# A conv-attention layer and a mixture-of-experts layer in one kernel: branch to the end, one pool for both layers, norm factors by way of DRAM

## The chip, the cores and the metric

The kernel runs on one core of a Trainium2 chip. The metric is device microseconds of one execution. Of the engines, TensorE (PE) does the matrix products and transposes, VectorE (DVE) and ScalarE (ACT) the elementwise work, GpSimd (POOL) a little of it, and SyncE (SP) issues all DMAs from one queue, in program order.

## The reference

Eight images `x` of 256 channels by 32 x 32 pixels (1024 tokens) pass two layers, all in float32.

```python
# layer 0 (norm1, norm2: RMS over the channels, per pixel)
q, k, v = bn(conv1x1(rms(x), qkv_w))                  # 4 heads, q and k of 32, v of 64
a = softmax(q.T @ k * 32**-0.5)                       # per head, over 1024 keys
x = x + gamma1 * bn(conv1x1(v @ a.T + bn(dwconv3(v)), proj_w))
h = dwconv3(conv1x1(rms(x), pi_w))                    # 1024 channels
f = conv1x1(gelu(h[:512]) * h[512:], po_w)
x = x + gamma2 * irfft2(rfft2(f by 8x8 patches) * fft_p)
# layer 1, on tokens t = x transposed
z = layer_norm(t)
t = t + causal_softmax(z WQ^T (z WK^T)^T / 16) @ (z WV^T)
z = layer_norm(t)
w = softmax(mean_over_images(z) @ Wr + br)            # 8 experts, one weight per token
t = t + sum_e w_e * (relu(bn(relu(bn(z W1_e)) W2_e)) Wo_e)
```

## The kernel before

**Layer 0.** An image is a block of 128 partitions x 2 channel groups x 1024 tokens, called `t`. The parts of an image are generators that issue a few instructions at each step: `attend` (scores, exponentials, products), `project`, `norm2`, `hidden` (the first conv of the FFN and its depthwise taps), `mix` (the second conv), `spectrum` (the patch transforms, by products with fixed matrices, and the addition to `t`). While image b is in its attention, image b-1 is in its FFN. The order in which the steps of the generators alternate is written out by hand in four strings, one letter per step: `FIRST` for stage 0, `ORDER` for stages 1 to 6, `LAST` for stage 7, `TAIL` for the FFN of the last image. All instructions of PE, ACT, DVE and POOL pass through `InOrder` (so nearly all carry line 88) and keep the program's order; no scheduler moves them. A letter's place thus sets where an instruction stands in its engine's queue. In the strings `h` is a step of `hidden`, `a` of `attend`, `d` and `q` of the next image's norm and keys, `s` of `spectrum`, `n` of `norm2`. `ON_PE` names the channel groups of `hidden` whose taps run as diagonal products on PE and not on DVE.

**The norm's factors.** `rms_norm` (L565) works on halves of 512 tokens. The sum of squares becomes one factor per token, a column per 128 tokens; `factors` (L592) takes the root and splits the factor `a` into a rounded part and a rest, `turned` (L612) transposes both to rows `rT`, and `apply` (L618) spreads them over 128 partitions by four products with the selector `pick_n` into PSUM, tile `rbn`, and multiplies: `xn<-t,vec,rbn` on DVE.

**The softmax divisor.** `attend` (L761) goes by blocks c of 256 queries. `close` (L788) takes the sums `sm` over the keys into `ss`, `invert` the reciprocal `r`, tile `sr`; `split` (L801) makes `rh` and the rest `rl`, and `spread` (L805) brings them to the channels of each head by four products with `pick_r` into tile `rb`, with which `pu` is multiplied. The softmax does not subtract a maximum. For that reason sums and reciprocals are gathered in `accs`.

**The seam.** After the last image's `spectrum`, L1233 to L1239 test `accs` and leave the integer `bad`. Each engine loads it and branches: if it is set, `layer0_shifted` (L182) computes layer 0 again, with the maximum subtracted. Layer 1's pools are opened behind the branch.

**Layer 1.** `scores_matrix` (in `TAIL`) has folded WQ and WK to one matrix, stored to `at_d`. Behind the branch `load_t` reads the image back from `t_d`, `load_experts` (L1348) issues 24 weight loads, and `first_norm(0)`, `keys(0)` and `values(0)` run by themselves: sixteen transposes into `tpt` and eight `bn_stats`, the root on POOL, scaling, transposing back to `z`, then products `pk` and `pv`. From then on images overlap: `statistics` of the next image, whose factors `rmT` are stored to `rm_d` and read back over all partitions as `rb`, lie beside the causal scores `s<-kk,z` of the current one. The expert FFN follows, in halves of 512 tokens, PE with hardly a pause; of its eight experts the odd ones replace products of 2 x 2 blocks by seven.

Of the kernel before, what the change touches and what calls it, by code (L numbers as in the profile page):

```python
# [18 lines left out]
P = 128  # L19
# [32 lines left out]
for _name, _w in _VEC:  # L52
# [7 lines left out]
    "aahhahdhhahqahahqahdhqhhhahaqahhqaaqadqaaqaaaaqaqaqaqaaqaaahqkvrgvvrgvvgpvrvvggppppp"  # L60
)
ORDER = (
    "nhsnhhsndhhhnhssnhshahnhahhsnshshhshhssdhshhhhhhaadshhhqahhahqhhhdhhhhqhhhhhdqdhhhhqdhhh"
    "qhdhhhhqhhdhhhqhhhahhhqhdhdhhhhqhdhhhdhhqkhavhhrgvgrvgvgpvrpvvppgppv"
)
LAST = (
    "nhshnhhahsnhsanhhshshnanhahnshshhshahshsshahhahhssahahhhdhhdhhhahhhahhhhhhaahaahhhhahhha"
    "ahhaahhhhdahhhhhhhaahhhhahhahhhahahhhhhhphprgrhghrgppppg"
)
TAIL = (  # L70
    "nnsnssnsnsnsnhhshhhhshshxhhsshhhhshhxhhmhhhhhshhhxhhhhhhmhhmhhhhhhhhhhhhhhhhhhhhhhhhhxhh"
    "hh"
)

ON_PE = ((), (), (2,))
# [18 lines left out]
def conv_attn_hybrid_kernel(  # L94
# [352 lines left out]
    t = [None] * B  # L447
    with ExitStack() as l0:
# [7 lines left out]
        def load_x(b):  # L456
            t[b] = two.tile([P, KC, N], F32, tag="t", name="t", bufs=3)
            nc.sync.dma_start(t[b], xv[b])


        t[0] = two.tile([P, KC, N], F32, tag="t", name="t", bufs=3)
# [3 lines left out]
        qkvw = wpool.tile([P, KC, 2 * C], F32, name="qkvw")  # L465
# [46 lines left out]
        pick_n = wpool.tile([2 * nq, nq, P], F32R, name="pick_n")  # L512
# [13 lines left out]
        mhalf = const.tile([P, nq], F32, name="mhalf")  # L526
# [38 lines left out]
        def rms_norm(b, wname, xn, first=False):  # L565
# [26 lines left out]
            def factors(h):  # L592
# [11 lines left out]
                pool.tensor_tensor(a, y, mhalf, ALU.pow)  # L604
# [3 lines left out]
                pool.tensor_mul(a, a, y)  # L608
                pool.tensor_copy(r[:, 0, :].bitcast(F32R), a)
                pool.tensor_sub(r[:, 1, :].bitcast(F32R), a, r[:, 0, :])  # L610

            def turned(h):  # L612
                tr = ps_m.tile([2 * nq, P], F32, tag="mm", name="tr")
                pe.transpose(tr, r_of.pop(h).rearrange("p a b -> p (a b)"), ident)
                rT_of[h] = small.tile([2 * nq, P], F32R, tag="rT", name="rT", bufs=2)
                act.copy(rT_of[h], tr)

            def apply(h):  # L618
                rT = rT_of.pop(h)
                rb = ps_m.tile([P, HALF], F32, tag="mm", name="rbn")  # L620
                for i in range(nq):
                    pe.matmul(rb[:, i * P : (i + 1) * P], pick_n[:, i, :], rT, start=True, stop=True)
                hs = slice(h * HALF, (h + 1) * HALF)
                for k in range(KC):
                    dve.scalar_tensor_tensor(xn[:, k, hs], t[b][:, k, hs], col(wname, k), rb, ALU.mult, ALU.mult)
# [31 lines left out]
        def queries_keys(b):  # L657
# [8 lines left out]
            for g, h in ((0, 0), (1, 0), (1, 1), (0, 1)) if b == 0 else ((0, 0), (0, 1), (1, 0), (1, 1)):  # L666
                if g not in att[b]:
                    hi = one.tile([P, N], F32R, tag=f"hi{g}", name="hi")
                    lo = one.tile([P, N], F32, tag=f"lo{g}", name="lo")
                    att[b][g] = (hi, lo)  # L670
# [7 lines left out]
                if b == 0 and (g, h) == (1, 0):  # L678
                    st = att[b]["kst"] = one.tile([P, NH, N], F32R, tag="kst", name="kst")
                    for r in range(4):  # L680
                        eng, src = ((dve, hi.bitcast(F32)), (pool, lo))[r // 2]
                        for hd in range(NH):
                            eng.tensor_copy(
                                st[r * KD : (r + 1) * KD, hd, hs], src[hd * KD : (hd + 1) * KD, hs]
                            )
                elif b == 0:
                    stack(b, ((g, hs),))
                yield 1.7

        def stack(b, parts=((0, slice(0, N)), (1, slice(0, N)))):  # L690
            for g, part in parts:
                hi, lo = att[b][g]
                name = ("qst", "kst")[g]
                if name not in att[b]:
                    att[b][name] = one.tile([P, NH, N], F32R, tag=name, name=name)
                st = att[b][name]
                for r in range(4):
                    src = (hi, lo, hi, lo)[r] if g == 0 else (hi, hi, lo, lo)[r]
                    for hd in range(NH):
                        nc.sync.dma_start(  # L700
                            st[r * KD : (r + 1) * KD, hd, part].bitcast(F32),
# [3 lines left out]
        def values(b):  # L705


            vT = att[b]["vT"] = one.tile([P, NT, C], F32, tag="vT", name="vT")
# [40 lines left out]
        def v_conv(b):  # L749
            o = att[b]["o"] = one.tile([P, KC, N], F32, tag="o", name="o")  # L750
# [10 lines left out]
        def attend(b, at_once):  # L761
# [26 lines left out]
            def close(c, po, sm):  # L788
# [5 lines left out]
                rh = two.tile([P, QC], F32R, tag="rh", name="rh", bufs=1)  # L794
                rl = two.tile([P, QC], F32R, tag="rl", name="rl", bufs=1)
# [5 lines left out]
                def split():  # L801
                    act.activation(rh, r, AF.Copy, accum_out=accs[:, 1, b, c : c + 1])
                    pool.tensor_sub(rl, r, rh.bitcast(F32))

                def spread():  # L805
                    rb = ps_m.tile([P, NH // 2, QC], F32, tag="mm", name="rb")
                    for pair in range(NH // 2):
                        pe.matmul(rb[:, pair, :], pick_r[:, pair, :], rh, start=True, stop=False)
                        pe.matmul(rb[:, pair, :], pick_r[:, pair, :], rl, start=False, stop=True)
# [23 lines left out]
            while units:  # L833
# [3 lines left out]
                for c, j in now:  # L837
                    s = ps_s.tile([P, NH, QC], F32, tag="s", name="s")
                    for hd in range(NH):
                        pe.matmul(  # L840
                            s[:, hd, :], kst[:, hd, j * P : (j + 1) * P], qst[:, hd, c * QC : (c + 1) * QC], start=True, stop=True
# [191 lines left out]
        def spectrum(b):  # L1033
# [50 lines left out]
            if b + 3 < B:  # L1084
                load_x(b + 3)

# [109 lines left out]
        lin = one.tile([P, 4, KC, C], F32, tag="qst", name="lin")  # L1196
        for i, src in enumerate((wqT, wkT)):
            nc.sync.dma_start(lin[:, i], src.rearrange("(k p) o -> p k o", p=P))

        def scores_matrix():  # L1200
# [8 lines left out]
            for g in range(KC):  # L1209
# [4 lines left out]
            act.activation(lin[:, 0], pa, AF.Copy, scale=1.0 / math.sqrt(C))  # L1214
            nc.sync.dma_start(at_d, lin[:, 0])
            yield 1.7

# [7 lines left out]
                "x": groups_on_pe(B - 1, ON_PE[2]).__next__,  # L1225
            },
            TAIL,
        )
        for _ in spectrum(B - 1):
            pass  # L1230
# [10 lines left out]

    with tc.If(nc.values_load(bad[0:1, 0:1]) > 0):
        layer0_shifted()
# [7 lines left out]
    z_d = [dram.tile([P, KC, N], F32, tag=f"zd{b}", name=f"zd{b}") for b in range(B)]  # L1251
    u_d = [dram.tile([P, KC, N], F32, tag=f"ud{b}", name=f"ud{b}") for b in range(B)]
    wm = ctx.enter_context(tc.tile_pool(name="wm", bufs=1))
    wrs = wm.tile([P, KC, NE], F32, name="wrs")
    nc.sync.dma_start(wrs, wr.rearrange("(k p) e -> p k e", p=P))
    brs = wm.tile([1, NE], F32, name="brs")
    nc.sync.dma_start(brs, br)

    wT = wm.tile([4 * NE, N], F32R, name="wT")

    w_of = []
    for e in range(NE):
        w_of.append([])
        for name in ("w1", "w2", "wo"):
            w_ = wm.tile([P, KC, C], F32, tag=f"{name}_{e}", name=f"{name}_{e}")
            w_of[e].append(w_)

    nc.vector.tensor_scalar_mul(wrs, wrs, 1.0 / B)

    sel_ = wm.tile([4 * NE, NE, P], F32, tag="tz0", name="sel_")  # L1270
    nc.gpsimd.memset(sel_, 0.0)
    for half in range(2):
        nc.gpsimd.affine_select(
            out=sel_, in_=sel_, compare_op=ALU.not_equal, fill=1.0, base=-NE * half,
            pattern=[[-1, NE], [0, P]], channel_multiplier=1,
        )
    sel8 = wm.tile([4 * NE, NE, P], F32R, name="sel8")
    nc.gpsimd.tensor_copy(sel8, sel_)
    sums_of = [[None] * 3 for _ in range(NE)]

    def seven(e):

        return e % 2 == 1

    sums_d = dram.tile([NE, 3, P, 3, P], F32, name="sums_d")

    def weight_sums(space):


        for e in range(NE):  # L1290
            for l in (0, 1, 2) if seven(e) else (0, 2):
                w_ = w_of[e][l]
                if e == 0:
                    s_ = sums_of[e][l] = wm.tile([P, 3, P], F32, tag=f"ws{e}_{l}", name=f"ws{e}_{l}")
                else:
                    s_ = space.tile([P, 3, P], F32, tag="ws", name="ws", bufs=2)
                a11, a21, a12, a22 = (w_[:, k, g * P : (g + 1) * P] for k in range(KC) for g in range(KC))
                dve.tensor_add(s_[:, 0, :], a21, a22)
                yield
                dve.tensor_sub(s_[:, 1, :], s_[:, 0, :], a11)  # L1300
                yield
                dve.tensor_sub(a21, a11, a21)
                yield
                dve.tensor_sub(s_[:, 2, :], a12, s_[:, 1, :])
                if e:
                    nc.sync.dma_start(sums_d[e, l], s_)
                yield

    def column_sums(src, T):

        B4 = src.rearrange("p k (c n) -> p (k c) n", n=QC)
        dve.tensor_sub(T[:, 0:2, :], B4[:, 1::2, :], B4[:, 0:2, :])
        dve.tensor_add(T[:, 2, :], T[:, 1, :], B4[:, 0, :])
        dve.tensor_sub(T[:, 3, :], B4[:, 2, :], T[:, 2, :])
        return T

    feat_d = dram.tile([P, KC, HALF], F32, name="feat_d")

    def gate(h, sums, lg, rows_of):


        nt = NT // 2
# [775 lines left out]
```

## Time and profile before

| | us |
|---|---|
| median of 3 runs | 3111.69 (3111.09 to 3112.32) |
| profiled execution, whole time | 3112.39 |
| its span in the trace | 3110.4 |
| stage 0 of layer 0 (attention of image 0) | 48.36 to 149.40 |
| stage 1 | 149.40 to 289.92 |
| stages 2 to 6 | 146.55 each, 289.92 to 1022.70 |
| stage 7 | 1022.70 to 1169.00 |
| FFN of the last image | 1169.00 to 1286.00 |
| seam to layer 1's first scores | 1286.00 to 1326.30 |
| layer 1's attention | 1326.30 to 1877 |
| expert FFN and end | 1877 to 3110 |

A row of the stretches of time gives the window, its length, then the busy time and number of instructions of PE, PEld (the load of PE's stationary operand, beside the products), DVE, ACT and POOL, PE's granted clock as a share of full speed, the share of the DMA engines and their GB/s. A row of the timeline gives start, duration, engine, line and operation, with the tiles as out<-in, and in square brackets how long the engine stood idle and for what. Rows of the DMA issues give the queue, the number of issues, the size of one and the time from issue to landing. The busy shares of the whole span (PE 95%, DVE 79%) are means over stages with different limits, so stages have to be read one by one.

### The profile page before, as it was taken

Reading aid. Unit: us, or ns where it says so; the run is one execution under the profiler, and the core shown is the slowest. Engines: PE = TensorE matmul, PEld = TensorE weight load, DVE = VectorE, ACT = ScalarE, POOL = GpSimd, SP = SyncE. Lnnn points to the kernel's source line nnn. Section 1 sums busy time; section 2 is a strip of 40 time slices with the busy share of each in tenths; the row PEclk is TensorE's granted clock in tenths of the full one; section 3 lists DMA queues with packets and bytes.
Section 4 is the critical chain, followed back from the end, with each engine's and each line's share of the span. In section 5 each row is a group of like instructions: output and inputs, shape, how many; then the busy total and the mean of one; then the engine's idle time right before and its main releaser. Section 6 shows DMA issues by size and latency. Waiting matters only on the chain. (4 is left out here: it accounts for less than half of the span.)

```text
span 3110.4 us, 42740 instructions
## 1 busy us (share of the span) xinstructions
PE 2968.0 (95%) x17008; PEld 2023.4 (65%) x17008; DVE 2444.3 (79%) x3796; ACT 1411.8 (45%) x2187; POOL 333.0 (11%) x486
## 2 busy tenths in 40 slices
PE   7989999999999989599999988999999999999998
PEld 4555555656565645356656656778887777788877
DVE  4398989898989897556676655888888878888887
ACT  4556556565656553132223323444444444444443
POOL 2131111111111100012222320000000000000000
PEclk9999999999999999799999998999999999999999
DMA  3202020203021100402222213000000000000000
GB/s 117 55 1 55 28 55 28 57 27 82 7 77 30 40 8 17 138 34 96 81 80 93 84 55 106 21 21 21 21 28 21 21 21 21 21 21 21 21 8 14
DMA packets 52293, 136.22 MB, mean 44 GB/s; under 512 B 7750, under 2 KB 20726, under 8 KB 46454
## 3 DMA queue, kind: packets, MB, share of 16 engines
q1 hardware_dynamic: 52086, 133.41, 13.6%
q8 instruction: 136, 2.23, 0.3%
q14 instruction: 71, 0.58, 0.1%
HBM read 62.88 MB, written 37.99 MB: 32 GB/s over the span
## 5 line engine op out<-in xcount | busy, mean ns | idle before, releaser
L88 ACT ACTIVATE h<-h,bn_o,bn_s 128x512 f32<-128x512 f32 x384 | 308.6, 813 | 627.8 <-DVE h L88 627.7
L88 ACT ACTIVATE pT<-s 128x1024 f32<-128x1024 f32 x256 | 260.7, 1024 | 193.4 <-PE sums L88 133.7
L88 DVE SCALAR_TENSOR_TENSOR conv<-hpad,vec,conv 128x1024 f32<-128x1024 f32 x256 | 333.0, 1306 | 6.1
L88 DVE SCALAR_TENSOR_TENSOR x<-hpad,vec,x 128x1024 f32<-128x1024 f32 x248 | 317.6, 1286 | 16.3 <-ACT x L88 9.9
L88 PE MATMUL pm<-h,w 128*128 128x512 f32 (+1 forms) x768 | 321.6, 528 | 0.0
L88 PE MATMUL po<-pT,vT 128*32 128x256 f32 x4096 | 274.8, 386 | 4.0 <-ACT pT L88 3.0
L88 PE MATMUL ph<-xn,piw 128*128 128x512 f32 x512 | 240.2, 604 | 3.7 <-ACT x L88 2.3
L88 PE MATMUL s<-kk,z 128*128 128x512 f32 x512 | 236.7, 594 | 3.6 <-DVE pr L88 3.6
L88 PEld LDWEIGHTS pm<-h,w 128*128 128x128 f32 x768 | 147.1, 192 | 76.7 <-issue 62.8
L88 DVE TENSOR_TENSOR h<-pa,first 128x512 f32<-128x512 f32 x128 | 88.2, 689 | 134.7 <-PE pa L88 128.9
L88 PE MATMUL s<-qst,kst 128*128 128x256 f32 x1024 | 188.5, 318 | 0.8 <-ACT pT L88 0.5
L88 DVE TENSOR_TENSOR h<-h,wb 128x1024 f32<-128x1024 f32 x128 | 156.2, 1220 | 41.0 <-ACT h L88 41.0
L88 DVE SCALAR_TENSOR_TENSOR o<-vpad,pe_w,o 128x1024 f32<-128x1024 f32 x128 | 163.8, 1282 | 29.5 <-ACT o L88 26.6
L88 PEld LDWEIGHTS s<-qst,kst 128*128 128x128 f32 x1024 | 140.0, 191 | 58.0 <-issue 45.9
L88 PEld LDWEIGHTS po<-pT,vT 128*32 128x32 f32 x4096 | 115.5, 110 | 90.8 <-ACT pT L88 8.4
L88 DVE TENSOR_TENSOR h<-h,first 128x256 f32<-128x256 f32 x384 | 163.1, 425 | 13.3
L88 PEld LDWEIGHTS ph<-xn,piw 128*128 128x128 f32 x512 | 91.0, 189 | 115.0 <-issue 95.1
L88 PE MATMUL sums<-pT,ones 128*32 128x256 f32 x2048 | 158.1, 380 | 0.0
L88 PE MATMUL pa<-tz,ws 128*128 128x256 f32 x512 | 154.9, 384 | 0.0
L88 PE MATMUL q<-t,ws 128*128 128x256 f32 x512 | 152.6, 380 | 0.8 <-DVE t L88 0.8
L88 PE MATMUL pa<-tz,w 128*128 128x256 f32 x512 | 153.0, 381 | 0.0
L88 PE MATMUL q<-t,wo 128*128 128x256 f32 x512 | 151.8, 379 | 0.0
(290 smaller groups left out, 5717.0 us busy)
## 6 DMA issues: line engine op xcount, KB each, us to landing
rb<-rm_d SPq DMA_DIRECT2D x14, 1024.0 KB, 4.7
td<-t SPq DMA_DIRECT2D x8, 1024.0 KB, 4.3
t<-td SPq DMA_DIRECT2D x8, 1024.0 KB, 6.7
te<-ud SPq DMA_DIRECT2D x16, 512.0 KB, 4.0
out_dram<-te SPq DMA_DIRECT2D x16, 512.0 KB, 3.2
ze<-zd SPq DMA_DIRECT2D x15, 512.0 KB, 3.9
t<-in_x_dram SPq DMA_DIRECT2D x7, 1024.0 KB, 6.3
qst<-hi SPq DMA_DIRECT2D x56, 128.0 KB, 2.3
```

The source lines that it names most:

```text
L88: return self._tc.keep_in_program_order(method(*args, **kwargs))
```

## The change

1. The branch goes to the very end. Layer 1 becomes a function `layer1(xp, shared, ahead)` and follows layer 0 at once; if `bad` is set, `layer0_shifted` and layer 1 are run again after everything else.
2. Both layers take `t`, the keys, `z`, the values and the first weights from one pool `xp` that is opened before layer 0; layer 0's `hi`/`lo`, stacked keys, `vT` and `o` use the same buffers. `load_t` of images 0 to 2 is issued in layer 0, after the `spectrum` of images 5 to 7. Layer 1's other pools are opened with `reuse_waits="tile"`: each tile waits for the tiles whose memory it takes over, not for the whole pool.
3. The former `first_norm(0)`, `keys(0)`, `values(0)` become `first_image()`, letter `l` in `TAIL`, and the last image's `spectrum` becomes letter `z` there.
4. Norm factors (but for image 0's first norm) are stored to DRAM from `rT` and read back over 128 partitions into SBUF, one buffer; POOL no longer splits them. The softmax divisors of the first three of four query blocks go the same way, four rows out and two reads back, each over 64 partitions.
5. The order strings are written anew, and the last image's group on PE is 6 and not 2.

```diff
-ON_PE = ((), (), (2,))
+ON_PE = [[], [], [6]]
...
+    xp = shared.enter_context(tc.tile_pool(name="xp", bufs=1, side="right"))
+    def load_t(b):
+        t[b] = xp.tile([P, KC, N], F32, tag="t", name="t1", bufs=3)
+        nc.sync.dma_start(t[b], t_d[b])
...
             def turned(h):
-                tr = ps_m.tile([2 * nq, P], F32, tag="mm", name="tr")
...
+                if not first:
+                    r_d = dram.tile([n, P], F32, tag=f"r{wname}{b}{h}", name="r_d")
+                    nc.sync.dma_start(r_d, rT_of.pop(h))
+                    rT_of[h] = one.tile([P, HALF], F32, tag="rbn", name="rbn")
+                    nc.sync.dma_start(rT_of[h], r_d.rearrange("a p -> (a p)").partition_broadcast(P))
...
             def apply(h):
-                rT = rT_of.pop(h)
-                rb = ps_m.tile([P, HALF], F32, tag="mm", name="rbn")
-                for i in range(nq):
-                    pe.matmul(rb[:, i * P : (i + 1) * P], pick_n[:, i, :], rT, start=True, stop=True)
+                rb = rT_of.pop(h)
+                if first:
+                    rT, rb = rb, ps_m.tile([P, HALF], F32, tag="mm", name="rbn")
+                    for i in range(nq):
+                        pe.matmul(rb[:, i * P : (i + 1) * P], pick_n[:, i, :], rT, start=True, stop=True)
...
                 def split():
-                    act.activation(rh, r, AF.Copy, accum_out=accs[:, 1, b, c : c + 1])
-                    pool.tensor_sub(rl, r, rh.bitcast(F32))
+                    to = both[:, 0, :] if on_pe else ss
+                    act.activation(to, r, AF.Copy, accum_out=accs[:, 1, b, c : c + 1])
+                    if on_pe:
+                        pool.tensor_sub(both[:, 1, :], r, both[:, 0, :].bitcast(F32))
+                        return
+                    r_d = dram.tile([NH, QC], F32, tag=f"rd{b}{c}", name="r_d")
+                    nc.sync.dma_start(r_d, r[0 : P : KD, :])
+                    for i in range(2):
+                        src = r_d.rearrange("(a i) n -> i a n", i=2)[i : i + 1].to_broadcast([HD, NH // 2, QC])
+                        nc.sync.dma_start(both[i * HD : (i + 1) * HD], src)
...
             if b + 3 < B:
                 load_x(b + 3)
+            else:
+                load_t(b + 3 - B)
+                begun.add(b + 3 - B)
...
+        def first_image():
...
+            for i0 in range(0, NT, 2):
+                tp = bank([P, 2, C])
+                for i in range(2):
+                    for k in range(KC):
+                        c0 = (i0 + i) * P
+                        pe.transpose(tp[:, i, k * P : (k + 1) * P], t[0][:, k, c0 : c0 + P], ident)
+                act.copy(zt[:, i0 : i0 + 2, :], tp)
+                yield
+                st = two.tile([P, 2, 6], F32, tag="pu", name="st", bufs=1)
+                for i in range(2):
+                    dve.bn_stats(st[:, i, :], zt[:, i0 + i, :])
+                    dve.bn_aggr(mv[:, i0 + i, :], st[:, i, :])
+                yield
...
                 "x": groups_on_pe(B - 1, ON_PE[2]).__next__,
+                "z": spectrum(B - 1).__next__,
+                "l": first_image().__next__,
             },
             TAIL,
         )
-        for _ in spectrum(B - 1):
-            pass
...
-    with tc.If(nc.values_load(bad[0:1, 0:1]) > 0):
-        layer0_shifted()
...
-        for _ in first_norm(0):
-            pass
-        for steps in (keys(0), values(0)):
+            for steps in () if ahead else (first_norm(0), keys(0), values(0)):
             for _ in steps:
                 pass
-        load_t(2)
...
+    layer1(xp, shared, True)
+
+
+    with tc.If(nc.values_load(bad[0:1, 0:1]) > 0):
+        layer0_shifted()
+        shared = ExitStack()
+        xp = shared.enter_context(tc.tile_pool(name="xpg", bufs=1, side="right"))
+        layer1(xp, shared, False)
```

## The prediction

> **What bounds the kernel now.** I read the page's totals and slices first, then the stretches stage by stage, then the timeline of the seam, then single rows.
>
> ```profile
> PE 2968.0 (95%) x17008; PEld 2023.4 (65%) x17008; DVE 2444.3 (79%) x3796; ACT 1411.8 (45%) x2187; POOL 333.0 (11%) x486
> PE   7989999999999989599999988999999999999998
> PEclk9999999999999999799999998999999999999999
> ```
>
> PE is the bound nearly everywhere, with dips in the FFN of layer 0's last image and at the seam (slices 15 to 17; the clock falls there too). The stretches say how much is to be had where:
>
> ```profile
> 289.92:436.48 146.56, 144.40 (x1214) 85.70 (x1213) 135.22 (x128) 88.70 (x136) 22.81 (x32) 1.00 0.17 44
> 1022.70:1169.00 146.30, 131.58 (x1137) 76.33 (x1136) 130.37 (x122) 77.73 (x112) 11.30 (x18) 0.95 0.03 12
> 1190.50:1270.90 80.40, 65.25 (x194) 35.42 (x192) 78.53 (x71) 27.27 (x46) 0.00 (x0) 0.94 0.04 17
> 1286.00:1326.30 40.30, 20.42 (x80) 14.90 (x81) 7.47 (x26) 8.69 (x15) 7.25 (x13) 0.75 0.80 276
> ```
>
> A middle stage (first row) is bound by PE, idle 2.2 of 146.6 us, with DVE 11.3 idle close behind. The last image's taps (third row) are bound by DVE, idle 1.9 of 80.4, while PE has 15 us free. The seam (fourth row) has PE at half, at a clock of 0.75. Its timeline:
>
> ```profile
> 1270.86 1.29 DVE L88 TENSOR_TENSOR hid<-x,conv 128x512 f32<-128x512 f32 x2
> 1285.90 0.14 DVE L1239 TENSOR_SCALAR bad<-votes 1x1 int32<-1x1 f32 x1
> 1292.64 0.39 SPq L1255 DMA_DIRECT2D wrs<-in_wr_dram  x1
> 1299.34 3.49 PE L88 MATMUL tpt<-ident,t 128*128 128x128 f32 x16 [13.92 <-DMA t<-td]
> 1312.74 7.03 PE L88 MATMUL pk<-z,at 128*128 128x512 f32 x16
> 1326.51 1.88 PE L88 MATMUL s<-kk,z 128*128 128x512 f32 x4
> ```
>
> From the last tap's end (1270.8) to layer 1's first scores (1326.5) pass 55.7 us: hid, mix and spectrum 15.1, branch 6.7 up to SP's first issue, image load 6.7, norm 13.4 (1299.3 to 1312.7), keys 6.9, values 6.9. The pieces form one chain, with no other work beside it.
>
> **The change, part by part.**
>
> *Seam.* Branch and load leave the chain: `load_t(0)` is issued a stage earlier. What stays behind the last tap is hid 0.75, the second half of mix up to 1277.0, 5.4, the spectrum up to the votes, 8.2, and what the new `TAIL` leaves of keys and values: in the new order of PE's instructions three pk tiles stand before the last mix, one pk and two pv between mix and spectrum, two pv behind it. By 6.9/4 a tile that is 5.2 + 3.4. Sum 23.0; some of it falls into the spectrum's own pauses (PE waits for `gf` and `t` in pieces of 0.2 to 1 us), so I take 22. Saved: 55.7 - 22 = 33.7.
>
> The transposes, norm and three pk tiles move into the taps' stretch. PE's part is 3.5 + 3.5 + 5.2 = 12 of its 15 free us: covered, but not if PE must wait for them in its order. DVE has no room: eight pairs of statistics at 0.53 and eight scalings at 0.33 (pitches in the old seam) make 7.0, all on the bound. Group 6 instead of 2 on PE leaves as many taps on DVE. So -7.0.
>
> SP: old, the image's load comes first and 24 weight loads are issued from 1296.6 to 1316.6, long before image 1's factors (rm_d at 1340.9, 14.4 behind the first scores; the multiplication at 1347.5, 21 behind). New, `load_t(2)` waits for the store of the last image (td<-t 4.3 us), which holds the queue; 20 weight loads at 0.83 follow, then rm_d and rb. Queue free: about 16.6 + 4.3 - 4 = 17 behind the first scores, with weights still on the way: the multiplication at 27. Of these 6 us scores of image 0 hide some; I take -4, between 0 and -6. `wrs` waits for the last `t` on DVE in front of them, which costs nothing as long as that `t` ends the layer anyway. Net of the seam 33.7 - 7.0 - 4 = 22.7.
>
> *Norm factors.* Marginal price on PE, from the start of the first product to that of the next other work:
>
> ```profile
> 506.29 0.38 PE L88 MATMUL rb<-rh,pick_r 128*128 128x256 f32 x1
> 506.86 0.50 PE L88 MATMUL ms<-pick_m,part 128*128 128x2 f32 x4
> 518.50 0.66 PE L88 MATMUL rbn<-rT,pick_n 8*128 8x128 f32 x4
> 519.09 0.27 PE L88 MATMUL tr<-ident,r 128*8 128x128 f32 x1
> L88 DVE SCALAR_TENSOR_TENSOR xn<-t,vec,rbn x64: 739/742/749, 17.4 to 1185.9; 128x512 f32<-128x512 f32 x64
> ```
>
> Four rbn products cost 0.59 us, four rb products 0.57. A middle stage loses 4 x 0.59 + 3 x 0.57 = 4.1 us of PE. On DVE, xn reads SBUF instead of PSUM: the taps (1.29 us for 1024 columns, all SBUF) suggest 0.66 instead of 0.742, 8 x 0.08 = 0.6 a stage. POOL loses two of seven instructions a half; it is idle anyway (22.8 of 146.6). ACT has as many instructions as before.
>
> In exchange each factor makes two dependent DMAs. The nearest rows:
>
> ```profile
> rm_d<-rmT SPq DMA_DIRECT2D x14, 8.0 KB, 1.3
> lin<-in_wqT_dram SPq DMA_DIRECT2D x1, 256.0 KB, 2.6
> ```
>
> About 1.5 + 2.6 = 4.1 us per trip, seven trips a stage, 17 DMAs at 0.4 us of SP. In the new order the pairs stand before the store of `t` and before the stacking's 32 DMAs, and the new `ORDER` puts steps between `turned` and `apply`. But there is one rbn buffer: the second half's read waits for the first half's `apply`, and everything behind it in SP's queue waits as well. The first to feel a late trip are `xn` on DVE, then `ph` or `pq` on PE. Bounds for a middle stage: 5.5 saved (4.1 and some of the 2.2 idle by the better order) and, with a third of the 28.7 us of trips exposed, 9.6 - 4.1 = 5.5 lost. I take 3.5 saved, nearer to the first, since the trace has 11 us of idle DVE in a stage and a step of any letter is a few tenths to 2 us long, so that a trip spans a handful. Five middle stages: 17.5.
>
> Stage 0 has only the second norm and the attention's three: 2 x 0.59 + 3 x 0.57 = 2.9, of which 2.0. Stage 1 has DVE at 130 and PE at 129 of 140.5 and waits that neither explains: 0.5. Stage 7 and the start of the tail are bound by DVE and by waits at their end: 2.0 (half of 4.1). Sum 4.5.
>
> *Layer 1's pools.* A wait per tile can start the expert FFN sooner:
>
> ```profile
> ACT first L88 <- DMA ud<-t: 10.7, 1, 10.7
> 1878.15 3.03 DMA ud<-t
> ```
>
> The first row is in the waits around 1878, the second the same wait in the chain that ended last. ACT's first output there waits for the whole store of the last image only because its memory was in the old pool. I credit the chain's 3.0; bounds 0 (another buffer has the same memory) and 3.7, PE's own wait there.
>
> *The branch at the end.* The last output is issued at 3106.5 and lands 3.2 us later, at 3109.7. The new load of `bad` stands behind that issue in SP's queue. How dear is a branch?
>
> ```profile
> L1242 SPq TENSOR_LOAD <-bad x1: 520/520/520, 1286.4 to 1286.4; - x1
> ```
>
> The load ended at 1286.9 and the next issue began at 1292.6: 5.7 us of jump. Behind 3106.9 come 0.5 + 5.7, end 3113.1, 3.4 past the landing: -3.4. The Trainium skill, "Advanced Engine Details and Errata", section "Control Flow Timing", puts a compare-and-branch at about 108 ns; by that the end would cost nothing (0.6 us beside a DMA of 3.2) and the total be 3.4 better. Its page "Runtime: NRT & Kernel Launch", section "Instruction fetch mechanics", speaks the other way: a taken branch that leaves the fetched pages must load them first. The 5.7 us side with the second, and the body jumped over at the end is larger yet; I use the trace's figure. Bounds 0 and -7.
>
> *Sum.* 22.7 + 17.5 + 4.5 + 3.0 - 3.4 = 44.3. The profiled execution took 3112.39, so 3068.1; the median of the runs is 0.7 lower: 3067.
>
> **The rivals.**
>
> *Forecast, 0.42:* as worked out, 3067, by itself 3057 to 3077.
>
> *DVE takes over in the stages, 0.22.* With 4.1 us less PE the stages lie at 142.5 against DVE's 135, and each late factor lands on DVE. For it: DVE busy 19.4 to 19.7 of 20 us in parts of the stage; against it: 9 us of its idle time is waiting for PE, which shrinks too. The trips eat the gain of all stages: 44.3 - 22 = 22, 3089.
>
> *The new orders bring more, 0.20.* Stage 7 idles PE 14.7 us and stage 1 11.7, with a clock of 0.95; if new `LAST` and `FIRST` fill 7, and the middle stages give 5.5 each (+10), 3050.
>
> *The seam stays half a chain, 0.12.* `first_image` stands between taps in fixed order; a transpose that waits for DVE's scaling holds `pz` and the diagonals behind it. If 12 us of the 33.7 reappear as waits within the taps, 3079. Here belongs also that the change does not do what it says, with layer 1's first instructions still held by pool memory at the seam: 22 us less, 3089.
>
> *Slower, 0.04: the factors' round trips are exposed.* Place: `apply` in stages 1 to 7, behind the single rbn buffer and SP's one queue, where a store of `t` waits for the last spectrum step and holds a trip behind it. All else gives 44.3 - 20 = 24.3. The sign turns when each of the seven stages is 24.3 / 7 = 3.5 us longer than before, that is with 3.5 + 4.7 (PE's and DVE's savings) = 8.2 of the 28.7 us of trips exposed. With half exposed, 14.3 - 4.7 = 9.6 a stage, 3112.4 - 24.3 + 67 = 3155. Against it: only the xn wait, not each trip, reaches the bound, and other letters lie between.
>
> **How the numbers follow.** The likeliest case gives 3067. The range takes in its own bounds, the case of more gain below and that of DVE-bound stages above: 3042 to 3092. A difference of under 0.2%, 6.2 us, can't be told from none by this measurement. All cases but the last are faster by more; between them and it lies a narrow strip: 0.94 faster, 0.02 same, 0.04 slower.
>
> **What would show it.** In the stages: the period falls from 146.56 to about 143 and PE's busy time to 140.3; a new row "DVE xn waits for DMA rbn" of under 1 us a stage says right, several us say the second or the last case. At the seam: from the last tap to the first `s` about 22 us instead of 55.7, no gap of PE for `t<-td`, the taps' stretch some 7 longer; image 1's factors about 27 behind the first scores. At 1878 the wait for ud<-t is gone. At the end some 3.4 us between the output's landing and the span's end. The forecast is wrong if the stages are no shorter, or if the taps' stretch grows by over 15.

## The result and the profile after

The changed kernel takes 3086.97 us (median of 4 runs, 3082.89 to 3087.98) against 3112.01 for the kernel before (4 runs): a ratio of 0.9917, 95% interval 0.9902 to 0.9933. The gain is 25 us where 44 were forecast. Its profiled execution took 3087.98 us with a span of 3086.3, 24.1 less than before. By stretches (stages are counted from one first `o<-vpad,pe_o` on ACT to the next):

| | before | after | change | forecast |
|---|---|---|---|---|
| start and stages 0, 1 | 289.92 | 282.33 | -7.6 | -2.5 |
| stages 2 to 6 | 732.78 | 732.23 | -0.6 | -17.5 |
| stage 7 and the last taps | 248.2 | 251.5 | +3.3 | +5.0 |
| last tap to layer 1's first scores | 55.7 | 23.2 | -32.4 | -33.7 |
| layer 1's attention, to the wait for the store ud<-t | 551.6 | 559.2 | +7.5 | +4 |
| expert FFN, to the last DVE operation | 1227.1 | 1230.5 | +3.4 | -3.0 |
| end | 5.1 | 7.3 | +2.2 | +3.4 |

The page's totals and slices:

```profile
PE 2953.0 (96%) x16792; PEld 2000.6 (65%) x16792; DVE 2434.1 (79%) x3796; ACT 1411.1 (46%) x2187; POOL 309.3 (10%) x401
PE   8999999999999988899999989999999999999998
PEclk9999999999999999999999988999999999999999
```

216 PE instructions have gone (the products that spread the factors). The dip of PE and of its clock at the seam is gone too. The stretches that answer to those shown before (window, length, then busy time and instructions of PE, PEld, DVE, ACT, POOL; clock, DMA share, GB/s):

```profile
428.50:575.18 146.68, 143.48 (x1186) 83.11 (x1185) 134.00 (x128) 88.60 (x135) 20.07 (x21) 0.99 0.22 57
1014.56:1160.86 146.30, 134.52 (x1142) 78.88 (x1141) 128.83 (x122) 78.50 (x115) 12.71 (x21) 0.94 0.08 28
1185.70:1266.00 80.30, 62.17 (x202) 35.46 (x202) 75.13 (x85) 28.74 (x49) 6.49 (x7) 0.91 0.09 33
1266.00:1289.20 23.20, 22.70 (x101) 15.75 (x99) 7.63 (x15) 5.56 (x10) 3.58 (x5) 1.00 0.08 31
```

The last row is the new seam: PE busy 22.7 of 23.2 us at full clock. The first is a middle stage: 28 PE instructions fewer (1214 to 1186), PE's busy time 0.9 us less and DVE's 1.2, and the stage as long as ever. The seam in the timeline:

```profile
1266.03 1.29 DVE L88 TENSOR_TENSOR hid<-x,conv 128x512 f32<-128x512 f32 x2
1289.25 1.98 PE L88 MATMUL s<-kk,z 128*128 128x512 f32 x4
1289.36 0.15 DVE L1347 TENSOR_SCALAR bad<-votes 1x1 int32<-1x1 f32 x1 [2.62 <-PE votes L1345]
```

Layer 1's first scores start beside the test of the sums, and nobody waits for it.

### The profile page after: what moved, and what is told of

It reads as the page before. It is cut to its first block, busy times and chain, and to the rows that moved or that the text cites. A ratio compares the mean times of both kernels' runs of the same rounds, so it can differ in the third digit from the quotient of the medians.

```text
span 3086.3 us, 42455 instructions
## 1 busy us (share of the span) xinstructions
PE 2953.0 (96%) x16792; PEld 2000.6 (65%) x16792; DVE 2434.1 (79%) x3796; ACT 1411.1 (46%) x2187; POOL 309.3 (10%) x401
## 4 chain that ended last, share of the span: by engine, by line
PE 53%; DVE 4%; DMA 1%; ACT 1%; issue 0%; SPq 0%; DVEq 0%; ACTq 0%
PE pm L88 13%; PE pa L88 13%; PE q L88 12%; PE s L88 5%; PE po L88 4%; PE pv L88 1%; DVE z L88 1%; PE pk L88 1%; PE tp L88 1%; PE tpt L88 1%; DVE h L88 1%; DVE pr L88 1%; DVE t L88 1%; DVE nm L88 1%; PE pz L88 0%; PE first L88 0%
## 5 line engine op out<-in xcount | busy, mean ns | idle before, releaser
L88 DVE SCALAR_TENSOR_TENSOR x<-hpad,vec,x 128x1024 f32<-128x1024 f32 x256 | 325.8, 1280 | 11.2 <-ACT x L88 4.3
L88 DVE SCALAR_TENSOR_TENSOR conv<-hpad,vec,conv 128x1024 f32<-128x1024 f32 x248 | 314.7, 1276 | 4.7
L88 PE MATMUL s<-qst,kst 128*128 128x256 f32 x1024 | 203.9, 331 | 3.6 <-ACT pT L88 3.5
L88 PEld LDWEIGHTS s<-qst,kst 128*128 128x128 f32 x1024 | 146.2, 196 | 84.4 <-issue 66.7
```

What stands on the lines that cost most here:

```text
L88: return self._tc.keep_in_program_order(method(*args, **kwargs))
```

## Experiments

Three questions: why the middle stages gained nothing, what the seam's 32 us are made of, and why layer 1 gave 8 back. The expectations name their theories by letters. In a middle stage: A, DVE is the bound; B, the new `ORDER` costs at the head of the stage what the round trips by way of DRAM bring; C, the trips hold the stage and only the new strings hide them; D, PE is the bound; E, PE and DVE are two tracks of nearly one length; F, a third chain sets the stage.

### What bounds a middle stage

Two edits, each in both kernels, and both edits together in the changed one.

```diff
 # relief_dve, relief_dve_before
-                    tap(dst, pad, dw_w[:, n, :], k)
+                    if alone or k != 8 or m >= 4:
+                        tap(dst, pad, dw_w[:, n, :], k)
 # relief_pe, relief_pe_before
-                for hd in range(NH):
+                for hd in range(NH if j % 2 == 0 else 0):
...
-start=(j == 0), stop=(j == nj - 1)
+start=(j == 0), stop=(j == nj - 2)
```

> The kernel before with the same half of the softmax-sum products left out, 9.8 us of PE less in a stage. The prediction read PE as the bound of the old middle stages (144.4 of 146.6 busy): then they fall to some 140, where DVE would take over, total about 3075. Theory A, in its stronger form (DVE was the bound before as well): 146 to 146.5, total 3105 to 3112.

> The kernel before with the same four taps a stage left out, 5.1 us of DVE less. If PE was the bound before: stages 145.5 to 146.5, total within 5 us of 3112. If DVE was: 141.5 to 142.5, total 3080 or less. If both, in turns: between, 143 to 145.

> The changed kernel with half of the softmax-sum products left out (every second key block): 16 x 0.61 = 9.8 us of PE less in a stage. Theory A: stages shorter by no more than 1 us, total 3078 to 3087. Theory D: stages 137 to 138, total about 3020.

> The changed kernel with one of the nine taps left out in four of the eight channel groups of each image but the last: 4 x 1.28 = 5.1 us of DVE less in a stage. Theory A (in the middle stages DVE is the bound, 134 us of work and 12 of idle at the head): stages 141 to 142, total about 3050. Theory D (PE is the bound after all, its waits hidden in the modelled durations): stages as in the changed kernel, 146 to 146.5, total 3085.

> The changed kernel with both left out: the four taps (5.1 us of DVE a stage) and half of the softmax-sum products (9.8 us of PE). Alone the taps gave nothing (146.2) and the products 0.8 (145.4). Theory E (two tracks of nearly one length: PE's work with its waits, and DVE's work with about 10 us of idle that it spends at the head of each stage waiting for PE and ACT): together they give what the shorter of them allows, 140 to 141 a stage, total about 3045. Theory F (a third chain of fixed length, DMA or ACT, sets the stage): 145 again, total about 3070.

Measured, one run each (length of the five middle stages, whole time):

| | stages | us |
|---|---|---|
| before | 146.55 to 146.56 | |
| relief_dve_before | 146.56 to 146.57 (five to 0.01) | 3109.55 |
| relief_pe_before | 144.85 to 144.88 | 3091.65 |
| changed | 146.17 to 147.01 | |
| relief_dve | 146.20 to 147.01 | 3084.44 |
| relief_pe | 145.35 to 147.50 | 3070.55 |
| relief_both | 142.47 to 142.96 | 3051.03 |

One stage of each of the three kernels that show it, as a stretch: the old one with four taps less,

```profile
578.48:725.04 146.56, 144.41 (x1214) 85.68 (x1213) 130.54 (x124) 88.82 (x136) 22.55 (x32) 1.00 0.17 44
```

the old one with half of the sums left out,

```profile
571.04:715.92 144.88, 138.85 (x1086) 81.43 (x1085) 134.88 (x128) 88.08 (x136) 24.95 (x32) 1.00 0.17 44
```

and the new one with both:

```profile
555.01:697.57 142.56, 135.55 (x1058) 77.94 (x1057) 128.88 (x124) 88.64 (x135) 18.02 (x21) 1.00 0.21 58
```

The old stage was PE's: DVE's work can shrink by 5 us and the length stays at 146.56. But 9.8 us of PE less (by the pitch of the products left out; PE's busy time falls by 5.6 in the rows), more than twice what the change takes away, gave 1.7: at 144.9 another track takes over. In it DVE is busy 134.9 and idle 10, and most of the idle part is no reserve. The waits of `relief_pe_before` in that stage show DVE, in the first 31 and the last 4 us of the stage, waiting for ACT's first `o` and for PE's `pf`, `py` and `pp`, each time the newest product of another engine:

```profile
DVE o L88 <- ACT o L88: 2.5, 1, 2.5
DVE gf L88 <- PE pf L88: 2.4, 1, 2.4
DVE t L88 <- PE pp L88: 1.8, 2, 1.0
DVE t L88 <- PE py L88: 1.0, 1, 1.0
```

(Columns: who waited for whom, us in total, times, longest.) So theory A is refuted as it was put (taps alone free nothing), and theory D too (9.8 us of PE are worth 0.8 to 1.7). By the median stage, both together brought 3.7 in the changed kernel where each alone brought 0 and 0.8: theory E, two tracks of nearly one length, and F, a third chain that holds all, is out at 145. For the old kernel the second track is read from DVE's waits; both edits together were not run there. E's number was missed, 142.5 against 140 to 141; with both left out PE is idle 7 and DVE 13.7, and what holds the stage there was not settled.

### Strings and factors, each alone

`old_strings` puts the old FIRST, ORDER and LAST into the changed kernel; `pe_factors` takes all factors back to PE; `pe_factors_old_strings` does both.

```diff
 # pe_factors: in rms_norm, where on_pe is set to True, and in close
-                if first:
+                if on_pe:
...
-                on_pe = c == N // QC - 1
+                on_pe = True
```

> The changed kernel with the strings FIRST, ORDER and LAST of the kernel before; factors still by way of DRAM, TAIL new. The middle stages took 146.2 us in the changed kernel and 146.55 before. Theory A (DVE is the bound: 134 us of work, and idle only at a stage's head): with the old strings 146 to 147, total within 5 us of 3087. Theory B (the new ORDER costs at the stage's head, where PE waits 2.0 us for POOL's r): the old strings give 143 to 144, total 3070 to 3075. Theory C (the new strings hide the round trips, and the old ones don't): over 148, total above 3095.

> The changed kernel with all factors spread by products on PE again, new strings. Theory A (DVE is the bound): the 4.1 us of products fall into idle time of PE, stages 146.5 to 148, total 3087 to 3095. Theory B (the new ORDER costs what the DRAM trips bring): stages about 150, total 3105 to 3110. Theory C (the round trips hold the stage): 143 to 145, total 3070 to 3080.

> The changed kernel with factors on PE and the strings FIRST, ORDER and LAST of the kernel before: what is left is the seam, the pools, TAIL and the branch at the end. All theories: stages as before, 146.55 (a difference would be the shared pool's). If the seam is nearly all of the gain, total 3088 to 3095 (29 saved from stage 7 to the first scores, some 13 given back in layer 1 and at the end, stages 0 and 1 without their 6).

| | middle stages | us | ratio to before |
|---|---|---|---|
| PE factors, old strings | 146.46 to 146.48 | 3100.92 | 0.9965 (0.9951 to 0.9979) |
| DRAM factors, old strings | 147.64 to 148.66 | 3103.24 | 0.9976 (0.9966 to 0.9986) |
| PE factors, new strings | 161.25 to 163.50 | 3190.0 | 1.0254 (1.0237 to 1.0271) |
| DRAM factors, new strings (the change) | 146.17 to 147.01 | 3086.97 | 0.9917 (0.9902 to 0.9933) |

With the old strings the DRAM factors cost a middle stage 1.2 to 2.2 us; the new strings bring it back to 146.2 and no further, where the forecast for both together was 143. In one stage of `old_strings` (428.77 to 576.41) DVE waits 3.6 us for the reads, against 1.4 in the changed kernel:

```profile
DVE xn L88 <- DMA rb<-r_d: 2.5, 1, 2.5
DVE xn L88 <- DMA rbn<-r_d: 1.1, 1, 1.1
```

Of the theories, C came nearest for `old_strings` (over 148), and B is refuted (143 to 144). Where the DRAM factors do pay is stages 0 and 1: with the old strings these take 97.6 and 136.0 us, and 100.9 and 140.1 with the products on PE (one trace each). No theory had the third row: the new strings are good only for factors by DMA. The first row was expected at 3088 to 3095; it came out higher as the old LAST and the products on PE cost 9 us from stage 7 to the first scores (283.8 against 274.7). With PE's products, DVE stands before `pu` and PE before `tr`; from the waits of one stage (623.55 to 786.70) of `pe_factors`:

```profile
DVE pu L88 <- PE rb L88: 11.7, 3, 7.2
DVE gf L88 <- PE pf L88: 7.5, 3, 5.2
PE tr L88 <- POOL r L88: 3.8, 2, 3.6
```

In the changed kernel the round trips themselves are near the estimate of 4.1 us. From the timeline of a stage's head, second norm of the first half and then of the second:

```profile
443.03 0.26 SPq L632 DMA_DIRECT2D r_d<-rT  x1
444.21 0.34 SPq L634 DMA_DIRECT2D rbn<-r_d  x1
446.37 0.26 SPq L632 DMA_DIRECT2D r_d<-rT  x1
447.23 1.42 DVE L88 SCALAR_TENSOR_TENSOR xn<-t,vec,rbn 128x512 f32<-128x512 f32 x2 [0.95 <-DMA rbn<-r_d]
448.67 0.32 SPq L634 DMA_DIRECT2D rbn<-r_d  x1
```

Out, in and landed in 4.2 us, 0.95 of them exposed; the second read is issued only when the first half's `xn` is through (448.65), as the single buffer has it. Ahead of it stands a new wait of 2.0 us, PE's `tr` for the last of five operations of POOL: the new ORDER calls `turned` with fewer scores in between.

```profile
435.47 1.73 POOL L88 TENSOR_TENSOR a<-y,mhalf 128x4 f32<-128x4 f32 x1 [16.67 <-ACT y L88]
437.21 6.43 DVE L88 SCALAR_TENSOR_TENSOR o<-vpad,pe_w,o 128x1024 f32<-128x1024 f32 x5
437.27 2.60 POOL L88 TENSOR_TENSOR y<-y,a 128x4 f32<-128x4 f32 x2
442.44 0.27 PE L88 MATMUL tr<-ident,r 128*4 128x128 f32 x1 [1.97 <-POOL r L88]
443.43 0.56 POOL L88 TENSOR_TENSOR y<-y,a 128x4 f32<-128x4 f32 x2
444.40 0.69 DVE L88 TENSOR_TENSOR gf<-pf,filt 128x512 f32<-128x512 f32 x1 [0.75 <-PE pf L88]
```

`pf` stands behind `tr`, so DVE's `gf` waits too. What this costs the stage is not shown: in `old_strings` PE has no such wait, and the stages are longer.

### The seam

`no_if_before` leaves the branch out of the old kernel. `first_image_after` leaves `first_image` out of TAIL and runs it behind everything, still ahead of layer 1.

```diff
 # no_if_before
-    with tc.If(nc.values_load(bad[0:1, 0:1]) > 0):
-        layer0_shifted()
 # first_image_after (TAIL without its letters l)
-                "l": first_image().__next__,
...
             TAIL,
         )
+        for _ in first_image():
+            pass
```

> The kernel before with the branch left out, load of bad included, nothing else changed. If the seam's cost is its chain and the branch is one link of 6.7 us, the first scores come 6 to 8 us earlier, total 3103 to 3106; if the branch also holds back the image load and the weights, which could start while layer 0 ends, up to 15 earlier, total about 3097. Leaving it out at a price of a compare-and-branch of 0.1 us and a load of 0.5 would give 1.

> The changed kernel with first_image taken out of TAIL: norm, keys and values of layer 1's first image run by themselves again, but behind the last spectrum at once, with the image long loaded and the pools shared. In the changed kernel 23.2 us pass from the last tap to the first scores, 55.7 before. If the overlap is what the seam's gain comes from: hid, mix and spectrum 14.4, norm 13.4, keys and values 13.8 make 41.6, less 7 in the taps' stretch where DVE is free of the norm, net 11 us slower than the changed kernel, total 3096 to 3100. If the early load and the shared pool are most of it and the overlap little (its instructions delay the taps by what they save later): under 4 us slower, total 3085 to 3091.

Without the branch the old kernel takes 3113.76 us, ratio 1.0007 (0.9998 to 1.0016): nothing. The issues of SP and PE's first transposes in that run:

```profile
1282.90 0.14 DVE L1239 TENSOR_SCALAR bad<-votes 1x1 int32<-1x1 f32 x1
1283.34 0.46 SPq L1083 DMA_DIRECT2D td<-t  x1
1288.84 0.34 SPq L1364 DMA_DIRECT2D t<-td  x1
1294.21 3.85 PE L88 MATMUL tpt<-ident,t 128*128 128x128 f32 x16 [11.78 <-DMA t<-td]
```

The image load is issued 5.9 us behind `bad`, 7.9 with the branch; from `bad` to the first scores pass 39.6 us against 40.6. The load comes 5.5 us behind the issue of the last store, which lands in about 4.3, and some weight loads have gone ahead of it. That it waits for that store because its pool lies in the same memory was not tried by itself. So the 6.6 us of the branch stood beside another wait, and taking it away alone earns 1 us.

`first_image_after` takes 3092.43 us, 0.9942 (0.9926 to 0.9959), 5.5 above the changed kernel:

```profile
1257.12 1.29 DVE L87 TENSOR_TENSOR hid<-x,conv 128x512 f32<-128x512 f32 x2
1300.17 1.88 PE L87 MATMUL s<-kk,z 128*128 128x512 f32 x4
```

From the last tap (1257.1) to the first scores 43.1 us, forecast 41.6; 55.7 before, 23.2 in the changed kernel. Branch, early load and shared pool are thus worth 12.6 together, the overlap 19.8. But the overlap is paid for in the taps: from stage 7's start to the last tap 239.2 us without it and 251.5 with it, 12.2 where I had 7.0. And without it stage 7 and the taps are 8.9 shorter than in the kernel before, where I had 2.0. Net, the overlap brings 7.6 at the seam.

Layer 1 takes even that back. From first to last scores pass 511.6 us without the overlap, as in the kernel before (511.5), and 519.6 with it, for the reason that the next part gives. The changed kernel's lead in the traces, 4.9 us, lies in parts that the edit leaves alone: 2.9 in the middle stages, 2.0 behind the last scores, 0.4 in the start and stages 0 and 1. As the changed kernel stands, the overlap has earned nothing.

### What layer 1 gave back

> The changed kernel with the 24 loads of the expert weights issued behind the read of image 1's factors instead of ahead of it. If the weights ahead in SP's queue and in the DMA engines are what holds those factors (rm_d issued 17.9 us behind the first scores and 5.4 us on the way, multiplication 27.9 behind), the multiplication comes 20 to 22 behind the first scores and the total falls by 5 to 8 us, to 3079 to 3082. If something else holds them, no change.

```diff
 # weights_late: in to_all_rows, behind the read
+                if b == 1:
+                    load_experts()
 # weights_late2: in beside, and rm_d, rb of image 1 and the weights in a fixed order on SP
                     turned(b + 1)
                     to_all_rows(b + 1)
+                    if b == 0:
+                        load_experts()
```

`weights_late` (3083.98 us, 0.9911, 0.9894 to 0.9927) was not the experiment meant: `to_all_rows` runs for image 1 twice, so the loads were issued twice, the second time over tiles already in use, which changes the expert FFN's weights; and SP still issued several of the first loads ahead of the factors. It says nothing on the cause.

> The changed kernel with the 24 loads of expert weights issued behind the read of image 1's factors, in a fixed order on SP. If the weights ahead in the queue hold those factors: multiplication 20 to 22 behind the first scores instead of 27.9, no drop of the clock there, total 5 to 8 us lower, 3079 to 3082. If the wait only moves to the weights (their sums on DVE stand beside image 1), no gain.

3080.33 us, 0.9903 (0.9886 to 0.9919). Image 1's factors in the changed kernel, and then in `weights_late2`:

```profile
1307.10 0.33 SPq L1579 DMA_DIRECT2D rm_d<-rmT  x1
1312.46 0.34 SPq L1584 DMA_DIRECT2D rb<-rm_d  x1
1317.07 0.69 DVE L88 TENSOR_TENSOR z<-t,rb 128x512 f32<-128x512 f32 x1 [6.49 <-DMA rb<-rm_d]
```

```profile
1306.08 0.32 SPq L88 DMA_DIRECT2D rm_d<-rmT  x1
1307.48 0.33 SPq L88 DMA_DIRECT2D rb<-rm_d  x1
1312.71 0.69 DVE L88 TENSOR_TENSOR z<-t,rb 128x512 f32<-128x512 f32 x1
```

The first scores start at 1289.25 and 1291.46: the multiplication comes 27.8 and 21.2 behind them. The store is issued 17.9 and 14.6 behind them, and from its issue to that of the read pass 5.4 us with the weights in flight and 1.4 without. `weights_late2` also fixes the order of these DMAs on SP, but `first_image_after`, which does not and whose weights are all issued by 1295.7, says the same: 1.4 us, and the multiplication 21.1 behind its first scores.

```profile
1314.62 0.33 SPq L1579 DMA_DIRECT2D rm_d<-rmT  x1
1316.02 0.34 SPq L1584 DMA_DIRECT2D rb<-rm_d  x1
```

In the changed kernel PE had two gaps of 2.7 us, and the clock of the 10 us that begin behind the first and hold the second was 0.71 (the third column from the end):

```profile
1318.54 1.12 PE L88 MATMUL pk<-z,w_l 128*128 128x512 f32 x2 [2.73 <-DVE z L88]
1325.41 2.41 PE L88 MATMUL s<-kk,z 128*128 128x512 f32 x4 [2.65 <-DVE pr L88]
1319.20:1329.20 10.00, 7.14 (x14) 3.03 (x13) 8.73 (x17) 3.02 (x5) 0.80 (x1) 0.71 0.01 2
```

In `weights_late2` the same stretch, counted from the first scores, has PE busy throughout at a clock of 1.00:

```profile
1321.40:1331.40 10.00, 9.97 (x28) 5.27 (x29) 4.16 (x9) 3.46 (x5) 1.71 (x2) 1.00 0.90 289
```

From first to last scores pass 519.6 us in the changed kernel, 511.8 here, 511.5 before: the whole 8 us. Of the kernels that compute the whole layer this is the fastest by its median; the intervals of the two ratios overlap, so that it is these stretches of the traces, not the totals, which show the cause.

## Why the prediction was right, and where not

The sign and the range held (3042 to 3092). The likeliest value was 20 us too low, and the result lies outside the forecast case's own 3057 to 3077. Step by step:

- *Seam, 33.7.* Right: 32.4, by the chain and the counts of tiles named. Its parts fit too: branch and load 13.4 of the old chain, measured 12.6; the overlap 20.3, measured 19.8.
- *The norm on DVE, -7.0.* Too small: the overlap lengthens the way to the last tap by 12.2. The pitches were right: DVE is busy 6.0 us longer there. Its idle time has grown by 6.2 as well (from 27.0 to 33.2), which the sum put at nothing; in the taps' stretch PE's wait for `hid` is 15.4 us with the overlap and 7.5 without. By luck it did not show in the total, as *stage 7, 2.0,* was too small by about as much: 8.9. With the old strings the DRAM factors bring 3.2 us there, and the new `LAST` another 5.4.
- *Image 1's factors, -4.* Mechanism and place right (forecast 27 behind the scores, measured 27.8), the price 8. I let half of the delay hide in scores; it hid nothing, as the gaps also cost clock.
- *Middle stages, 3.5 each.* This step failed, and with it 17 us: the stage is 0.1 shorter on the mean, and "the stages are no shorter" was the prediction's own sign of being wrong. It was not the sign that it watched for in DVE: `xn` waits 0.9 us for its read, under the 1 us named. The products are gone, but PE's busy time fell to 141.7 to 143.5 and not to 140.3. I took DVE's 11 us of idle time as room for a late factor and as the distance to the next bound. The runs show a second track at 144.9, only 1.7 below PE's, so that 4.1 us of PE alone could bring no more than that. Nor is DVE's idle time all waiting for PE: of the 9 us of waits 6 are for PE and 3 for ACT.

  What became of the 1.7 is known in part: the trips cost 1.2 to 2.2 with the old strings, which the new ones win back. In the stage shown DVE's work fell by 1.2 us and its idle time rose by 1.3. The work fell in the taps (`conv` from 1306 to 1273 ns), not in `xn` as forecast, which took 0.746 us from SBUF and 0.742 from PSUM. The waits for `gf` rose from 2.4 to 3.8 us. Which of these waits holds the changed stage stays open.

  The rival "DVE takes over in the stages" had size and time (3089), in part by luck, as it takes the gains of stages 0, 1 and 7 away too; that DVE alone decides is refuted.
- *Stages 0 and 1, 2.5.* Measured 7.6, too small a forecast. The start and these two stages vary: in `no_if_before`, which has the old layer 0, they end at 286.7 and not 289.9. But the two pairs of stages above differ by 7.4 through the factors alone. Stage 0 is PE's: half of the sums left out shortened it from 98.6 to 90.8.
- *Layer 1's pools, 3.0.* Nothing: the lower bound held. The wait for ud<-t went from ACT to DVE, as a row of the waits shows (the chain has 3.33 us for it, 3.03 before):

```profile
DVE h L88 <- DMA ud<-t: 3.6, 1, 3.6
```

  The FFN's 3.4 lost lie in its first 100 us, at a clock of 0.88 against 0.93. From the last scores to the last output the kernels of this study spread by 6 us, the four with the old layer 1 by 4, so that nothing is laid to the change here.
- *End, -3.4.* Right in kind, 2.2 by the trace. The last output is issued at 3080.2, and behind it SP loads the condition and branches:

```profile
L2086 SPq TENSOR_LOAD <-bad x1: 496/496/496, 3080.6 to 3080.6; - x1
L2086 SPq COMPARE_BRANCH  x1: 50/50/50, 3081.2 to 3081.2; - x1
L2086 SPq EVENT_SEMAPHORE  x8: 17/17/17, 3084.3 to 3084.9; - x8
```

  The branch instruction takes 0.05 us, and SP's next one comes 3.1 us behind it; closing instructions follow up to 3086.3. The 5.7 us that the prediction carried over held more than this. In the old place SP's own gap is 3.1 us too (1287.4 to 1290.6); ACT, POOL and DVE stand still for 5.6 us behind their branches, and SP then waits for a semaphore up to 1292.5. Of the prediction's two readings of a branch the dear one holds, at a smaller price; that the 3.1 us go into loading instructions, no run shows.

## What to carry to other kernels

An engine's idle time is no reserve before it is known what it waits for; take work away from each engine in turn, then from both, and see which length moves. A wait taken away alone can earn nothing (the branch). What one part gains, the next can give back: the overlap's 7.6 us went into layer 1, because the first scores came forward and the weights did not. An order of instructions written for one latency can be ruinous for another (161 us a stage). Where a small transfer that the next stage waits for shares queue and DMA engines with bulk loads, issue it first: the loads of 6 MB here could wait, the 8 KB could not.

## What was not expected of the hardware

- Small POOL operations slow down beside DVE's work. `y<-y,a` (128x4) took 0.20 us wherever DVE stood idle, and up to 1.28 beside its SCALAR_TENSOR_TENSOR; so the chain of five took 6.9 us in the first half of the stage shown and 2.2 in the second, whose last four operations fall for the most part into an idle stretch of DVE. POOL's own idle time does not explain it: `a<-y,mhalf` took 1.73 us after 16.67 us of idle, but 1.01 after 49.6 in `old_strings`. This is read from the start times; no run tried it by itself.
- In the kernels with round trips by way of DRAM the five middle stages of one execution differ by 0.5 to 2.6 us; with all factors on PE and the old strings they agree to 0.02. The trips are not the only cause: with all factors on PE and the new strings they differ by 2.3.
- With two gaps of 2.7 us on PE went a granted clock of 0.71 over 10 us. In the middle stages a dip of the clock cost nothing that can be seen: three of the five (0.99) have one, and on the mean they are no longer than the two at 1.00.
